# Last image's grams in groups of 32 tokens with turned copies half on VectorE, and fixed places for the second image's grams, in a two-layer attention and correlation kernel

## The chip, the cores and the metric

The kernel runs on one core of one Trainium2 chip. The metric is the device time of one execution in microseconds (us), given as the median of several runs. Profiles come from one further execution, with the hardware profiler on. A core has five engines with an instruction stream each: TensorE (PE in the profile; PEld is its weight loads), VectorE (DVE), ScalarE (ACT), GpSimd (POOL) and SyncE (SP), which here issues nearly all DMAs; SPq in the profile is its queue of DMA issues. Engines wait for each other through semaphores.

## The reference

Input x is 8 images of 768 channels and 32 x 32 tokens, float32. There are two residual layers, each ahead of it a GroupNorm over 32 groups.

```python
x = x + L0(gn(x))
x = x + L1(gn(x))
```

L0 is an attention of 12 heads (64 wide) in which the scores are the outer product of two vectors, the variances of v and of k over the head's 64 channels:

```python
scores = var(v, ddof=1) @ var(k, ddof=1).T * 64 ** -0.5
out = softmax(scores) @ v @ W_proj.T + b_proj
```

L1 divides every token's 768 channels by their norm, correlates each token with 28 neighbours, and puts the 28 correlations behind the 768 channels of a 1x1 convolution:

```python
norm = sqrt(sum(f * f, axis=1)); feat_n = f / max(norm, 1e-12)
corr = [sum(shift(feat_n, r - 3, c - 3) * feat_n, axis=1) for r, c in offsets]
out = einsum('bchw,oc->bohw', concat([f, corr], 1), conv_w) + conv_b
```

The offsets are the two diagonals, the middle row and the middle column of a 7 x 7 square.

## The kernel before, in words

Channels are split into J = 6 blocks of 128 partitions and the 1024 tokens of an image into 8 tiles t of 128 (four rows of 32). The program goes through the images one after the other: keys and values (matmuls `x`, `y`, `z` <- `kv`, L350), attention (`ex` on ScalarE L775, `av` on TensorE L801), the projection, and the 1x1 convolution of the image before (Strassen-like products `x`, `y`, `z` <- `wt`, whose operands `t1f`, `t2f`, `t4f` are made on VectorE). TensorE works through one hand-written order; the correlations of image b - 1 are put beside the keys, values and attention of image b. The last image has nothing beside it: its grams, correlations and products are the end of the program.

**The correlations** are in the class `Corr` (L1126 on). Four steps matter here.

- `turn(t)` (L1130) copies tile t of the feature map `f`, for each side (the left or right 16 columns), so that the 64 tokens of a side lie next to each other: two operations of 128 x 384 elements. For the last image ScalarE does both (`act_copy`, L229), into tiles of `expool` that the attention no longer uses; for the others GpSimd does (L1143), into `turnpool`, which has one buffer. So there turn t + 1 can start when gram t has read turn t.
- `gram(t)` (L1145) multiplies these copies by `f` itself: for each of 6 channel blocks and each side, 64 tokens by the 7 rows x 19 columns around them (133 columns; 76 for t = 7, which has only 4 rows left), added up in one PSUM tile `gr` (L1159). These tiles come from the pool `smp` with two buffers. After its matmuls it starts the turns of the next tile, or of the next two for the last image.
- `out()` (L1169), due 1.65 us later by the planner, copies `gr` into `win` (VectorE; ScalarE for the last image) and writes it to a DRAM buffer `windowed` with one DMA for each side (L1177), 64 partitions at a time. `wins` has two buffers in turns, and a third for t = 7.
- After every four tiles come `diagonals` (four DMAs `dd`, L1191, that read the needed products out of `windowed`), `scale` (`m`, `rn`, `dn`, a transpose `ct` on TensorE, `cr`, four DMAs `rows`, L1228), and after both halves `gather` (14 DMAs, L1239 to L1245, a product on VectorE, three DMAs `cs`<-`cs`, L1254). The matmuls `cc` (L1278, for the last image L1376) then use `cs`.

**What sets the order.** A planner (`Clock`) runs while the program is written: each unit of TensorE's work has a cost in us (`GRAM_US` 1.4, `KV_US` 1.93), and jobs on other engines are due so many us after a unit (`later.after`), or after the planner's VectorE (`later.after_dve`). What is due is written into the program when the planner's time has come, so a cost changes only the order in which instructions stand on each engine. On the chip nothing waits for the planner; each engine runs its instructions in that order.

The grams of image b - 1 are called by `next_to` (L1400), from the attention's steps and from places put into the list of key and value units: `rest.insert`, after 3 and 7 units for images from the third on, and for the second image (whose grams are those of the first) after 7, 12, 14, ... 28. `next_to` runs a gram only once `clock.now` has passed `clock.turned`, which `gram` sets to 1.4 + 2.3 us after its start. `remaining` (L1395) runs those that are left.

For the last image the list is: two product units, the eight grams one after the other, and then the other products, with the `cc` units between the last of them. VectorE meanwhile makes `t1f`, `t2f`, `t4f` and finishes the two products of the image that were set aside (`held<-z,held`, `f<-x,bconv_sb,f`).

Of the kernel before, what the change touches and what calls it, by code (L numbers as in the profile page):

```python
# [13 lines left out]
P = 128  # L14
NB, C, H, W = 8, 768, 32, 32
N = H * W
J = C // P
NH, HD = 12, 64
HP = NH // 2
MT = N // P  # L20
# [7 lines left out]
RUNS = ((0, 0, 4), (31, -1, 3), (62, -2, 5), (93, -3, 7))  # L28
HW = W // 2
TALL, WIDE = MT // 2 + 3, HW + 3  # L30
AHEAD_OF = [o for first, _, count in RUNS for o in range(first, first + count)][1:]
NA = len(AHEAD_OF)
PAD = 99
SPAN = TALL * WIDE
WIN = SPAN + 3
# [18 lines left out]
TAIL = 0.0  # L54
EXP, SUM, STEP_US = 1.07, 1.15, 1.73
KV_US, T_US, CORR_US = 1.93, 2.58, 1.2
GRAM_US, TURN_US = 1.4, 2.3
WARM, BRIDGE = 42, (3, 7)


# [31 lines left out]
class Clock:  # L92


    def __init__(self):
        self.now, self.count, self.jobs = 0.0, 0, []
        self.act, self.rows, self.poll = 0.0, ([], []), lambda: None
        self.dve = self.turned = 0.0

    def after(self, us, job):  # L100
        self.count += 1
# [71 lines left out]
def two_layers(ctx, tc, x, wkv, wproj, bproj, wconv, wcorr, bconv, out):  # L173
# [952 lines left out]
    class Corr:  # L1126
# [3 lines left out]
        def turn(self, t):  # L1130

            last = self.b == NB - 1
            pl, tag = (expool, "ex") if last else (turnpool, "turn")
            flat = pl.tile([P, N if last else J * P], F32, tag=tag, name=f"turn{self.b}_{t}")[:, : J * P]
            self.turned[t] = flat.rearrange("p (j s m) -> p j s m", j=J, s=2)
            to = flat.rearrange("p (j s y x) -> p j s y x", j=J, s=2, x=HW)
            rows = self.f[:, :, t * P : (t + 1) * P].rearrange("p j (y s x) -> p j y s x", y=4, s=2)
            for side in range(2):
                if last:
                    act_copy(0.5, to[:, :, side], rows[:, :, :, side, :])  # L1140
                else:
                    half = rows[:, :, :, side, :]
                    nc.gpsimd.tensor_tensor(to[:, :, side], half, windows(ones, ones.ap[0], (0, J), (HW, 4), (1, HW)), ALU.mult)  # L1143

        def gram(self, t):  # L1145

            b = self.b
            tall = min(TALL, H - 4 * t)
            n = tall * WIDE
            if t not in self.turned:  # L1150
                self.turn(t)
            clock.turned = clock.now + GRAM_US + TURN_US
            block = self.turned[t]
            ps = other([P, SPAN], f"gr{b}_{t}")
            for j in range(J):
                image = self.f[:, j, :].rearrange("p (y x) -> p y x", x=W)
                for side in range(2):
                    left = side * (HW - 3)
                    nc.tensor.matmul(  # L1159
                        ps[side * HD : (side + 1) * HD, :n].rearrange("p (y x) -> p y x", x=WIDE),  # L1160
                        lhsT=block[:, j, side, :],
                        rhs=image[:, 4 * t : 4 * t + tall, left : left + WIDE],
                        start=j == 0, stop=j == J - 1,
                    )
            for ahead in range(t + 1, min(t + (3 if b == NB - 1 else 2), MT)):
                if ahead not in self.turned:
                    self.turn(ahead)

            def out():  # L1169
                win = wins[t % 2 if t < MT - 1 else 2]  # L1170
                if b < NB - 1:
                    vector.tensor_copy(win[:, :n], ps[:, :n])
                else:
                    act_copy(0.3, win[:, :n], ps[:, :n])
                for side in range(2):
                    to = windowed[b % 2][t : t + 1, side * (HD * PITCH + HD - 3) :]
                    nc.sync.dma_start(  # L1177
                        out=windows(to, (HW * PITCH - 3, 4), (PITCH, HW), (1, WIN)), in_=win[side * HD : (side + 1) * HD, :]
                    )
                if t % 4 == 3:  # L1180
                    later.after(4.0, lambda: self.diagonals(t // 4))

            later.after(GRAM_US + 0.25, out)

        def diagonals(self, hf):

# [14 lines left out]
        def scale(self, hf, dd):  # L1201

            b = self.b
            m = st.tile([P, 4], F32, tag="m", name=f"m{b}_{hf}")
            vector.tensor_scalar(m, dd[:, :, 0], NORM_EPS2, None, ALU.max)
            rn = st.tile([P, 4], F32, tag="rn", name=f"rn{b}_{hf}")
            nc.gpsimd.tensor_tensor(rn, m, neghalf, ALU.pow)

            def columns():
                dn = st.tile([P, 4, NROW], F32, tag="dn", name=f"dn{b}_{hf}")  # L1210
                vector.tensor_copy(dn[:, :, 0], rn)
                for q in range(4):
                    vector.scalar_tensor_tensor(dn[:, q, 1:NROW], dd[:, q, :], rn[:, q : q + 1], mask, ALU.mult, ALU.mult)
                later.after_dve(0.7 if b else 5.0 if hf else 7.5, lambda: to_dram(dn))

            def to_dram(dn):
                pt = small(f"ct{b}_{hf}")
                columns, over = dn.rearrange("p q r -> p (q r)"), 4 * NROW - HD
                turned(pt[0:HD, 0:P], columns[:, 0:HD])
                turned(pt[HD:P, 0:P], columns[:, over:])  # L1220
                cr = work([P, P], f"cr{b}_{hf}")
                vector.tensor_copy(
                    cr.rearrange("k (y s x) -> k y s x", y=4, s=2),
                    pt[:, 0:P].rearrange("k (s y x) -> k y s x", s=2, y=4),
                )
                for q in range(4):
                    at, row = PAD + hf * HF + q * P, q * NROW + (HD - over) * (q == 3)
                    nc.sync.dma_start(out=rows[b % 2][:, at : at + P], in_=cr[row : row + NROW, :])  # L1228
                if hf == 1:
                    later.after(3.0, self.gather)  # L1230

            later.after_dve(2.5, columns)
# [161 lines left out]

    def remaining(beside):  # L1395
        while beside:
            clock.turned = 0.0
            next_to(beside)

    def next_to(beside):  # L1400

        if beside and ready.issuperset(beside[0][1]) and clock.now >= clock.turned:
            us, _, unit = beside.pop(0)
            unit()
            clock.pass_time(us)
# [146 lines left out]
    for b in range(NB + 1):  # L1552
# [8 lines left out]
        if b:  # L1561
            has_f = ("f", b - 1),
            if b > 1:
                clock.wait(*has_f, ready=ready)
            f, acc = layer1[b - 1] if b > 1 else first_f * 2
            corr = corrs.pop() if 1 < b < NB else Corr(b - 1, f) if b == NB else None
            conv = Conv(
                b - 1, f, images[b] if b < NB else acc, (lambda b=b: next_image(b + 1)) if b + 1 < NB else lambda: None
            )
            if b < NB:  # L1570

                def low_residual(b=b, f=f):
                    for n in range(JH):
                        later.after(1.5 * n, lambda n=n: nc.sync.dma_start(out=f[:, n, :], in_=xv[b, :, n, :]))

                conv.then = low_residual
            grams = [(GRAM_US if t < MT - 1 else 0.9, has_f if b > 1 else has_f + ("turned",), lambda t=t: (corr or corrs[0]).gram(t)) for t in range(MT)]
            first, start = (0.0, has_f, conv.sums.first), (0.0, (), conv.start)
            if b < NB:
                beside = grams  # L1580
                for n in (3, 7) if b > 1 else (7,) + tuple(range(12, 30, 2)):
                    rest.insert(n, (0.0, has_f, lambda: next_to(beside)))
                rest.insert(len(rest) - 4, (0.0, has_f, lambda: remaining(beside)))
                rest.insert(len(rest) - 4, first)
                rest += [start] + conv.units()
                if b == NB - 1:
                    rest.insert(len(rest) - 3, (0.0, (), conv.set_aside))
            else:
                units, parts = conv.units(), conv.corr_units()
                rest += [first, start] + units[:2] + grams + units[2:17]  # L1590
                for n, unit in enumerate(units[17:]):
                    rest += parts[n : n + 1] + [unit]
        else:
            more = [(us, (("xn", 1),) * (n > 1), unit) for n, (us, _, unit) in enumerate(kv1.units(0))]
            rest.insert(len(rest) - 3, (0.0, (), lambda: apply_second(0)))
            rest += [(0.0, (), lambda: apply_second(1))] + more[:20] + [(0.0, (), lambda: fill_t(3))] + more[20:]
            rest += [(0.0, (), lambda: fill_t(TBLOCKS - 3))]
# [51 lines left out]
```

## Time and profile before

| what | value |
| --- | --- |
| median of 3 runs | 2582.31 us (2581.68 to 2583.05) |
| the profiled execution: time | 2580.96 us |
| its span | 2579.2 us |
| TensorE busy in it | 2571.7 us, 14798 matmul instructions |
| VectorE / ScalarE / GpSimd busy | 1586.1 / 1418.3 / 424.4 us |
| last image's eight grams (first `gr` to first `y`) | 2510.96 to 2522.19 us of the span |
| mean granted TensorE clock | 1.000 |

How to read it: the span is the time from the first to the last instruction of the profiled execution, and every time inside the trace counts from its start. One float32 matmul of the program shows as two instructions of TensorE in the profile. A line such as `L350 PE MATMUL x<-kv,xn 128*64 128x384 f32 x1512 | 260.3, 486 | 0.0` is a group of instructions: source line, engine, operation, output and inputs by the program's names, shape (here 128 rows by 64 columns of weights, 384 columns moved), their number, total busy us, mean ns of one, and idle time of the engine ahead of them. Lines of a timeline have start us, duration us, what, the number of merged instructions, and in brackets the idle time ahead of it with what ended it. Matmuls are pipelined: one's duration is longer than the distance to the next one's start, so sums are made from start to start.

### The profile page before, as it was taken

Reading aid. Unit: us, or ns where it says so; the run is one execution under the profiler, and the core shown is the slowest. Engines: PE = TensorE matmul, PEld = TensorE weight load, DVE = VectorE, ACT = ScalarE, POOL = GpSimd, SP = SyncE. Lnnn points to the kernel's source line nnn. Section 1 sums busy time; section 2 is a strip of 40 time slices with the busy share of each in tenths; the row PEclk is TensorE's granted clock in tenths of the full one; section 3 lists DMA queues with packets and bytes.
Section 4 is the critical chain, followed back from the end, with each engine's and each line's share of the span. In section 5 each row is a group of like instructions: output and inputs, shape, how many; then the busy total and the mean of one; then the engine's idle time right before and its main releaser. Section 6 shows DMA issues by size and latency. Waiting matters only on the chain.

```text
span 2579.2 us, 40704 instructions
## 1 busy us (share of the span) xinstructions
PE 2571.7 (100%) x14798; PEld 1328.9 (52%) x14798; DVE 1586.1 (61%) x4101; ACT 1418.3 (55%) x1972; POOL 424.4 (16%) x449
## 2 busy tenths in 40 slices
PE   9999999999999999999999999999999999999999
PEld 5654356434764345643476434764347643575333
DVE  6868735775447853478534885358853577536864
ACT  1497279811697217971179711897118971189610
POOL 4320130004300043000430003300133001331000
PEclk9999999999999999999999999999999999999999
DMA  8766356355563655636556365563655636545333
GB/s 293 291 225 224 104 204 194 116 198 170 184 202 104 197 168 176 206 99 205 170 175 202 97 211 170 167 203 105 220 170 163 207 106 219 167 139 166 118 111 108
DMA packets 324718, 448.19 MB, mean 174 GB/s; under 512 B 59810, under 2 KB 245522, under 8 KB 324518
## 3 DMA queue, kind: packets, MB, share of 16 engines
q1 hardware_dynamic: 322454, 442.24, 53.1%
q10 hardware_dynamic: 2064, 3.34, 0.4%
q8 instruction: 118, 1.93, 0.3%
q14 instruction: 82, 0.67, 0.1%
HBM read 376.70 MB, written 64.40 MB: 171 GB/s over the span
## 4 chain that ended last, share of the span: by engine, by line
PE 97%; DMA 1%; ACT 1%; DVE 0%; SPq 0%; issue 0%; POOL 0%; ACTq 0%; POOLq 0%; DVEq 0%
PE x L350 34%; PE av L801 25%; PE y L350 17%; PE z L350 10%; PE own L350 5%; PE gr L1159 3%; PE den L832 1%; ACT ex L775 1%; PE warm L419 1%; DMA bc<-vdr 1%; ACT junk L785 0%; PE z L1064 0%; PE y L1064 0%; PE cc L1278 0%; DMA vdr<-rsv 0%
## 5 line engine op out<-in xcount | busy, mean ns | idle before, releaser
L775 ACT ACTIVATE ex<-bc,nk 128x1024 f32<-128x1024 f32 x768 | 826.9, 1137 | 398.8 <-DMA bc<-vdr 167.2
L801 PE MATMUL av<-ex,v 128*64 128x512 f32 x3072 | 694.2, 593 | 1.6 <-ACT ex L775 1.5
L801 PEld LDWEIGHTS av<-ex,v 128*64 128x64 f32 x3072 | 328.6, 137 | 322.7 <-issue 211.4
L785 ACT ACTIVATE junk<-bk,vm 128x1024 bf16<-128x1024 f32 x368 | 420.4, 1142 | 28.0 <-issue 10.7
L167 DVE TENSOR_TENSOR acc<-acc,ex 128x1024 f32<-128x1024 f32 x300 | 344.8, 1211 | 0.0
L350 PE MATMUL y<-kv,s 128*64 128x384 f32 x1488 | 265.3, 487 | 0.1
L350 PE MATMUL x<-kv,xn 128*64 128x384 f32 x1512 | 260.3, 486 | 0.0
L350 PE MATMUL x<-kv,s 128*64 128x384 f32 x1488 | 256.0, 486 | 0.0
L229 ACT COPY kp<-x 128x384 f32<-128x384 f32 x28 | 13.3, 478 | 404.7 <-PE x L350 395.9
L350 PEld LDWEIGHTS x<-kv,xn 128*64 128x64 f32 x1512 | 139.2, 137 | 104.6 <-issue 85.7
L350 PEld LDWEIGHTS x<-kv,s 128*64 128x64 f32 x1488 | 143.0, 137 | 92.7 <-issue 72.5
L350 PEld LDWEIGHTS y<-kv,s 128*64 128x64 f32 x1488 | 137.2, 137 | 88.6 <-issue 72.4
L530 POOL TENSOR_TENSOR rstda<-vea,neghalf 128x1 f32<-128x1 f32 x8 | 4.8, 595 | 950.8 <-DVE vea L167 950.8
L1143 POOL TENSOR_TENSOR turn<-f,ones 128x384 f32<-128x384 f32 x112 | 111.0, 1011 | 247.1 <-PE gr L1159 169.0
L350 PE MATMUL z<-kv,xn 128*64 128x384 f32 x768 | 134.2, 486 | 0.0
L350 PE MATMUL x<-f,wt 128*64 128x512 f32 x504 | 118.8, 592 | 0.0
L167 DVE TENSOR_TENSOR v<-y,v 128x128 f32<-128x128 f32 x180 | 40.9, 282 | 121.7 <-PE y L350 121.6
L636 POOL TENSOR_TENSOR s<-xn 128x384 f32<-128x384 f32 x64 | 65.0, 1026 | 293.3 <-PE x L350 181.7
L167 DVE BATCH_NORM_STATS2 vbn<-v 128x6 f32<-128x64 f32 x720 | 101.5, 209 | 0.0
L350 PEld LDWEIGHTS z<-kv,xn 128*64 128x64 f32 x768 | 75.0, 137 | 46.7 <-issue 36.1
L229 ACT COPY acc<-li 32x256 f32<-32x256 f32 x128 | 51.5, 402 | 82.9 <-DVE li L167 81.5
L1159 PEld LDWEIGHTS gr<-f,turn 128*64 128x64 f32 x1344 | 88.0, 136 | 11.9 <-issue 5.1
(205 smaller groups left out, 3132.5 us busy)
## 6 DMA issues: line engine op xcount, KB each, us to landing
kv<-kvs SPq DMA_DIRECT2D x124, 576.0 KB
kv<-in_wkv_dram SPq DMA_DIRECT2D x95, 576.0 KB
bc<-vdr SPq DMA_DIRECT2D x96, 512.0 KB
f<-in_x_dram SPq DMA_DIRECT2D x48, 512.0 KB
bk<-kdr SPq DMA_DIRECT2D x46, 512.0 KB
x1d<-f SPq DMA_DIRECT2D x42, 512.0 KB
xn<-x1d SPq DMA_DIRECT2D x42, 512.0 KB
out_dram<-xn SPq DMA_DIRECT2D x82, 256.0 KB
```

The source lines that it names most:

```text
L167: return getattr(self.engine, name)(*args, **kw)
L229: nc.scalar.copy(to, at)
L350: nc.tensor.matmul(out[at], lhsT=lhsT[:, at], rhs=rhs, start=start, stop=stop, **kw)
L419: nc.tensor.matmul(warm[:, 0:P], lhsT=ident, rhs=ident, start=True, stop=True)
L530: nc.gpsimd.tensor_tensor(self.rstd, ve, neghalf[:, 0:1], ALU.pow)
L636: nc.gpsimd.tensor_tensor(self.sums[g][:, 0], a[g][2], a[g][3], ALU.add)
L775: nc.scalar.activation(ex, self.bc[e], AF.Exp, scale=self.kv.nk[self.half][:, h, t : t + 1])
L785: nc.scalar.activation(junk, self.bk[e], AF.Exp, scale=self.kv.m2[self.half][:, h, t : t + 1], accum_out=self.sums[:, e, t : t + 1],)
L801: nc.tensor.matmul(self.av[hf][e * HD : (e + 1) * HD, :], lhsT=self.vt[:, t, e, :], rhs=exs[e][:, hf * HF : (hf + 1) * HF], start=t == 0, ...
L832: nc.tensor.matmul(den[at * 32 : (at + 1) * 32, :], lhsT=ones[:, 0:32], rhs=self.acc[e][:, hf * HF : (hf + 1) * HF], start=True, stop=True,)
L1143: nc.gpsimd.tensor_tensor(to[:, :, side], half, windows(ones, ones.ap[0], (0, J), (HW, 4), (1, HW)), ALU.mult)
L1159: nc.tensor.matmul(ps[side * HD : (side + 1) * HD, :n].rearrange("p (y x) -> p y x", x=WIDE), lhsT=block[:, j, side, :], rhs=image[:, 4 * ...
```

## The change

For the last image a gram is made in four groups of 32 tokens (two rows of one side) rather than two of 64. Each group needs only 5 rows x 19 columns = 95 columns of `f` rather than 133 (76 as before for t = 7), so there are 24 matmuls rather than 12 in a gram. The window of each group starts at its own first row, and for t = 0 to 6 `win` is written by four DMAs of 32 partitions (2 x 16 x 98 elements) rather than two of 64 (4 x 16 x 136). The turned copy of the right side (`side` 1) is made on VectorE rather than ScalarE. In the planner a gram of the last image is 0.3 us cheaper, its `out` is due 0.3 us earlier and its `to_dram` 1.7 rather than 0.7 us after its columns.

For all images the gate `clock.turned` is gone, and the second image's grams stand after 7, 11 and 15 units of its keys and values, with the others from the attention's steps and `remaining`.

```diff
+SHORT = 2 + 3
-GRAM_US, TURN_US = 1.4, 2.3
+GRAM_US = 1.4
...
             for side in range(2):
-                if last:
+                if last and side:
+                    vector.tensor_copy(to[:, :, side], rows[:, :, :, side, :])
+                elif last:
                     act_copy(0.5, to[:, :, side], rows[:, :, :, side, :])
...
         def gram(self, t):
             b = self.b
-            tall = min(TALL, H - 4 * t)
+            last = t == MT - 1
+            groups = 4 if b == NB - 1 else 2
+            tall = min(SHORT if groups == 4 else TALL, H - 4 * t)
             n = tall * WIDE
             if t not in self.turned:
                 self.turn(t)
-            clock.turned = clock.now + GRAM_US + TURN_US
...
-                for side in range(2):
-                    left = side * (HW - 3)
+                each = P // groups
+                for at in range(groups):
+                    side, low = divmod(at, groups // 2)
+                    left, first = side * (HW - 3), 4 * t + (0 if last else 2 * low)
                     nc.tensor.matmul(
-                        ps[side * HD : (side + 1) * HD, :n].rearrange("p (y x) -> p y x", x=WIDE),
-                        lhsT=block[:, j, side, :],
-                        rhs=image[:, 4 * t : 4 * t + tall, left : left + WIDE],
+                        ps[at * each : (at + 1) * each, :n].rearrange("p (y x) -> p y x", x=WIDE),
+                        lhsT=block[:, j, side, low * each : (low + 1) * each],
+                        rhs=image[:, first : first + tall, left : left + WIDE],
                         start=j == 0, stop=j == J - 1,
                     )
...
-                for side in range(2):
-                    to = windowed[b % 2][t : t + 1, side * (HD * PITCH + HD - 3) :]
+                whole = last or groups == 2
+                size, count, down = (WIN, 4, 0) if whole else (SHORT * WIDE + 3, 2, 2 * (HW * PITCH - 3 + WIDE))
+                for first in range(0, P, count * HW):
+                    side, low = divmod(first, HD)
+                    to = windowed[b % 2][t : t + 1, side * (HD * PITCH + HD - 3) + (down if low else 0) :]
                     nc.sync.dma_start(
-                        out=windows(to, (HW * PITCH - 3, 4), (PITCH, HW), (1, WIN)), in_=win[side * HD : (side + 1) * HD, :]
+                        out=windows(to, (HW * PITCH - 3, count), (PITCH, HW), (1, size)),
+                        in_=win[first : first + count * HW, :size],
                     )
...
-            later.after(GRAM_US + 0.25, out)
+            later.after(GRAM_US + 0.25 - (0.3 if b == NB - 1 else 0.0), out)
...
-                later.after_dve(0.7 if b else 5.0 if hf else 7.5, lambda: to_dram(dn))
+                later.after_dve((0.7 if b < NB - 1 else 1.7) if b else 5.0 if hf else 7.5, lambda: to_dram(dn))
...
     def remaining(beside):
         while beside:
-            clock.turned = 0.0
             next_to(beside)
...
-        if beside and ready.issuperset(beside[0][1]) and clock.now >= clock.turned:
+        if beside and ready.issuperset(beside[0][1]):
...
-                for n in (3, 7) if b > 1 else (7,) + tuple(range(12, 30, 2)):
+                for n in (3, 7) if b > 1 else (7, 11, 15):
```

More of the change, by code (lines that the diff above doesn't have):

```diff
@@ L97, in __init__ @@
         self.act, self.rows, self.poll = 0.0, ([], []), lambda: None
-        self.dve = self.turned = 0.0
+        self.dve = 0.0
     def after(self, us, job):
@@ L1576, in two_layers @@
                 conv.then = low_residual
-            grams = [(GRAM_US if t < MT - 1 else 0.9, has_f if b > 1 else has_f + ("turned",), lambda t=t: (corr or corrs[0]).gram(t)) for t in range(MT)]
+            grams = [(GRAM_US - (0.3 if b == NB else 0.0) if t < MT - 1 else 0.9, has_f if b > 1 else has_f + ("turned",), lambda t=t: (corr or corrs[0]).gram(t)) for t in range(MT)]
             first, start = (0.0, has_f, conv.sums.first), (0.0, (), conv.start)
```

## The prediction

> **What bounds the kernel now.** I read the totals first, then the chain of work that ended last, then the same chain in the stretch of the last image's grams, and then each engine's timeline there and in the second image. TensorE is busy for 2571.7 of 2579.2 us, and the page's chain says the same:
>
> ```profile
> PE 97%; DMA 1%; ACT 1%; DVE 0%; SPq 0%; issue 0%; POOL 0%; ACTq 0%; POOLq 0%; DVEq 0%
> ```
>
> So an edit counts only where it shortens TensorE's work or makes it wait. The chain from 2508 to 2530 us (start, us, what) is the last image's grams:
>
> ```profile
> 2511.12 2.75 PE gr L1159 x48
> ...
> 2517.91 0.28 ACT win L229
> 2518.19 0.02 issue
> 2518.21 0.52 SPq L1177
> 2518.72 0.05 issue
> 2518.78 2.15 DMA windowed<-win
> ...
> 2521.03 0.28 ACT win L229
> 2521.30 0.04 issue
> 2521.35 1.01 PE gr L1159 x24
> 2522.36 5.15 PE y L350 x24
> ```
>
> The reader is to see that this stage hangs partly on the windows: a copy to `win`, two issues 0.57 us apart (2518.21, 2518.78; the piece called DMA starts with the second), landing 1.63 us after the second ends, then the next copy into that buffer, which frees a PSUM tile for a gram. By start times on TensorE the grams run from 2510.96 to 2522.19 = 11.23 us. Seven grams at 1.36 and one at 0.79 make 10.31, so 0.92 us is waiting.
>
> **1. The shorter grams.** A pair of 64-column matmuls starts 113.3 ns after the last at 133 columns and 66 ns at 76; on that line 95 columns take 82 ns. A gram is then 12 rounds x 82 = 0.98 us, if four 32-column groups run beside each other as two 64-column ones do. The row for that form:
>
> ```profile
> 2420.40 1.06 PE L832 MATMUL den<-acc,ones 128*32 128x512 f32 x8
> ```
>
> Two rounds of four at 512 columns take 1.0 us (the rounds start 0.453 apart, the four within 20 ns), so the groups do run together; some 0.13 us goes on entering the form and as much on leaving. The eight grams would be 7 x 0.98 + 0.79 + 0.29 = 7.94 us: at best 3.3 us less than 11.23, with no waits left. The Trainium skill speaks against it: "TensorE: Matmul & The Clock Gate", section "Wait — 56ns, not 53.3ns?", has starts never closer than some 25 ns, which would make a round 100 ns and the best gain (my estimate from it) 1.7 us. The den records, 6.7 ns apart in a round, do not show that floor.
>
> **2. Half the turned copies on VectorE.** Before, ScalarE made the first turned copies while it had nothing else to do:
>
> ```profile
> 2508.43 3.40 ACT L229 COPY turn<-f_last 128x384 f32<-128x384 f32 x8 [49.85 <-DVE f_last L167]
> ```
>
> VectorE has no such gap (timeline, same stretch):
>
> ```profile
> 2511.26 0.74 DVE L167 SCALAR_TENSOR_TENSOR f<-x,bconv_sb,f 128x512 f32<-128x512 f32 x1
> 2511.92 1.88 DVE L167 TENSOR_TENSOR t2f<-f_last,t1f 128x512 f32<-128x512 f32 x3
> 2513.72 0.74 DVE L167 SCALAR_TENSOR_TENSOR f<-x,bconv_sb,f 128x512 f32<-128x512 f32 x1
> 2514.39 1.89 DVE L167 TENSOR_TENSOR t<-f_last 128x512 f32<-128x512 f32 x3
> ```
>
> In the new order on VectorE the first three copies stand behind t2f, that is at 2513.72, and everything ahead of it runs without a pause. A 128x384 copy takes 0.55 us (the mean of kp<-x, which reads PSUM); taken. Its bounds are 0.27, by a 128x1024 f_last at 0.72 to 0.81, and 0.93, the pair of ScalarE copies. So the copy is there at 2514.28, and gr_0, whose third matmul reads it, runs from about 2514.35 instead of 2510.96: **TensorE stands for 3.4 us**, which is all that the shorter grams can return. ScalarE's 8 x 0.41 us less is worth nothing by itself.
>
> **3. Four issues for each gram instead of two.** The queue's own rows (ns min/median/max):
>
> ```profile
> L1177 SPq DMA_DIRECT2D windowed<-win x128: 511/526/622, 354.3 to 2527.8; - x128
> L1228 SPq DMA_DIRECT2D rows<-cr x64: 294/322/1336, 396.7 to 2539.7; - x64
> L1243 SPq DMA_DIRECT2D cs<-rows x32: 231/270/288, 423.1 to 2547.9; - x32
> ```
>
> No row has the new shape (2x16x98). Bounds: 0.30 from start to start by cs<-rows, 0.62 by the slowest windowed. I take 0.55: it is a windowed write with one dimension shorter, so that row is nearest. Then SyncE needs 4 x 0.55 = 2.2 us for a gram against 0.98 of TensorE: **the queue becomes the bound of the stage.** gr_0 ends at 2514.35 + 0.98 + 0.13 = 2515.46; 0.51 us later (as between gr_0 and its first issue before) the first write is issued, 2515.97. The window of gram 5 goes into the buffer of gram 3, whose last issue ends 16 x 0.55 = 8.8 us later; landing, copy and release add 1.63 + 0.42 = 2.05, and gr_7 can start at 2526.82 where it started at 2521.35: **+5.5 us** on all that follows. At 0.62 it is +6.6; at 0.30 the landing of each buffer's writes sets the pace instead, first issue + 12 x 0.30 + 4.1, about +2.3.
>
> **4. Behind it.** The wt load and the four dd issues that stand behind 28 window issues are later, as is the ct transpose (to_dram due at 1.7, not 0.7; one pair of matmuls later). gather's last load lands near 2556 and is wanted near 2560. The cs product goes behind one more f<-z on VectorE; the copies of cs before landed at 2559.1 and the first cc started at 2561.35, and about 0.2 of this 2.25 us is left. Taken as nothing, at worst 0.5 us.
>
> **5. The second image.** With one buffer, turn t+1 starts only when gram t has read turn t. POOL's rows beside keys and values:
>
> ```profile
> 373.69 1.99 POOL L1143 TENSOR_TENSOR turn<-f,ones 128x384 f32<-128x384 f32 x2 [3.25 <-PE gr L1159]
> 375.63 1.97 POOL L636 TENSOR_TENSOR s<-xn 128x384 f32<-128x384 f32 x2
> ...
> 383.32 1.99 POOL L1143 TENSOR_TENSOR turn<-f,ones 128x384 f32<-128x384 f32 x2
> 385.25 1.04 POOL L1207 TENSOR_TENSOR rn<-m,neghalf 128x4 f32<-128x4 f32 x1
> 387.15 1.99 POOL L1143 TENSOR_TENSOR turn<-f,ones 128x384 f32<-128x384 f32 x2 [0.86 <-PE gr L1159]
> ```
>
> A gram's end to its turn takes 0.70, the turn 1.99, the next gram follows 0.06 later: 2.75 us to cover. With the gate gone gr_0, gr_1 and gr_2 each have one unit between them, y<-kv and then x<-kv, 1.935 us each: two stalls of 0.82. gr_3 to gr_5 have an attention step or two units (3.87) and are covered. turn_5 now stands ahead of the eight s operations (7.7 us) and turn_6 behind them, which I work out to leave gr_6 some 0.3 us short. On the other side ScalarE's order changes: two of its sums (junk, 1.27 each) move up, one into this wait for bc:
>
> ```profile
> 446.74 4.43 ACT L775 ACTIVATE ex<-bc,nk 128x1024 f32<-128x1024 f32 x4 [2.89 <-DMA bc<-vdr]
> ...
> 461.70 1.69 PE L801 MATMUL av<-ex,v 128*64 128x512 f32 x4 [0.24 <-ACT ex L775]
> ```
>
> ScalarE's six ex from 460.51 come 1.27 us earlier, and the 0.57 us that TensorE's starts lose ahead of the second line go. Sum: 2 x 0.82 + 0.3 - 0.57 = **+1.4 us**; bounds -0.6 (no stall) and +2.7 (the stalls, a longer one at gr_6, and no gain).
>
> **The sum.** 5.5 + 1.4 = +6.9 us on the profiled execution's 2580.96 (span 2579.2 and 1.76 around it) is 2587.9. That execution is 1.35 us under the median 2582.31, so against the median: **2589.2 us**, +0.27%. A measurement of this kernel can tell 0.2%, 5.2 us, from no change.
>
> **Rivals.**
> A. The smaller write is cheap to issue, 0.30 to 0.37 us: step 3 then gives +2.3 to +3.3, and with step 5 the sum is +1.5 to +5, about 2586. For it: three-row loads at 0.27. Against: the windowed row hardly varies (511 to 622 ns). The second image's stalls being covered (step 5 at -0.6 to 0) ends here too: 5.5 - 0.3 = +5.2 or less.
> B. TensorE, 45% busy in the queue-bound stage (0.98 of 2.2) after standing 3.4 us, loses its clock. The window at the end of the span (us, PE busy, ..., PEclk, DMA share, GB/s) has it:
>
> ```profile
> 2575.00:2579.20 4.20, 0.39 (x2) 0.00 (x0) 0.75 (x1) 0.00 (x0) 0.00 (x0) 0.85 0.18 68
> ```
>
> The records there go from full to half clock at 2577.98, 2.6 us after the last matmul. Two to three us of that clock fall under issues anyway; then some 3.4 to 6.8 us of Strassen products run at half speed, 1.7 to 3.4 us more: +8.6 to +11.7, about 2592. Against: each gap inside the stage is only 1.2 us. The skill's rule in Part 1 of the same page (half clock after an idle window of about 3.4 us, free-running) would give this or not by the phase of the window.
> C. Not slower: the copy on VectorE does not hold gr_0. Its place in VectorE's order decides; were turn_0 made ahead of t1f, as ScalarE's is (done by 2509.2), and an issue under 0.25 us (four of them under a gram's 0.98), 11.23 would become 7.94. With 461.70's 0.57 gained: -3.3 to -3.9 us, about 2578.7. Against: the order puts three operations and t2f ahead of it, and no issue row is that cheap.
>
> **Chances.** Forecast (+5.2 to +8.6) 0.55; A 0.24; B 0.13; C 0.08. The forecast and B are slower by over 0.2%: 0.68. A and half of C are within: 0.28. The other half of C, with gains that I do not see, is faster: 0.04. The range reaches from A's lower part (+1.7) to the end of B (+11.7): 2584.0 to 2594.0; it leaves out C and the ends of A and B, under 0.2. The forecast's own range is 2587.5 to 2590.9.
>
> **What would show it.** Right: gr_0's third matmul released by DVE turn near 2514.3; rows windowed x4 gapless on SyncE, 0.5 us or more each; grams near 1.0 us but 2.2 apart; y from about 2527.7; two waits for POOL turn of 0.8 us near 355 to 360. Wrong: windowed rows under 0.4; grams longer than 1.2; y before 2524; a PEclk under 1.00 between 2511 and 2535.

## The result, and the profile after

The changed kernel took 2586.98 us (median of 21 runs), the kernel before 2581.14 us (21 runs): ratio **1.0021, interval 1.0015 to 1.0028**, slower by 3.9 to 7.2 us. The profiled execution has a span of 2583.6 us (2579.2 before). It is the fastest of the 21 (2585.32 us), and its mean granted clock is 1.000; of the other 20 executions, two have 1.000, fifteen 0.999 and three 0.998.

To see where that comes from I took the start of every matmul in both traces and subtracted before from after, instruction by instruction. The difference is -0.96 us behind the warm-up (the granted clock rises to 1.00 at 5.66 us there, and at 7.75 in before) and -0.70 at 340 us, -2.02 at 350, -1.23 at 400, -2.0 to -2.2 from 470 to 2500, and +4.35 from the first y behind the last image's grams to the end. So +6.36 us arose in the last image's grams (6.21 between the first gram's start and the first y). In the second image +0.79 arose beside the keys and values and -0.84 near 461 us; the -1.32 between 342 and 350 lies ahead of every instruction that the change moves there (see e1 and e2).

The chain that ended last, in the last image's grams of the changed kernel (start us, us, what):

```profile
2511.79 0.28 DVE turn L168
2512.07 0.04 issue
2512.11 1.20 PE gr L1165 x46
...
2513.60 0.68 SPq L1186
...
2522.59 0.57 SPq L1186
2523.16 0.04 issue
2523.20 1.97 DMA windowed<-win
...
2525.27 0.25 ACT win L230
2525.51 0.04 issue
2525.56 1.00 PE gr L1165 x48
2526.56 5.30 PE y L351 x24
```

Between 2513.60 and 2523.16 it holds only issues on SyncE's queue, 15 of them; the 16th starts at 2523.20 and is the first part of the piece called DMA. They are those of four windows. Where before two issues stood in the chain between grams, now the queue is the chain. TensorE's waits from 2508 to 2530 us (waiting line, for what: us in total, times, longest) show the two costs side by side, and a short stop that comes back in e11 and e12:

```profile
PE gr L1165 <- ACT win L230: 5.0, 4, 1.3
PE gr L1165 <- DVE turn L168: 2.7, 1, 2.7
PE gr L1165 <- issue: 0.4, 1, 0.4
```

The timelines of VectorE and SyncE there:

```profile
2509.91 1.88 DVE L168 TENSOR_TENSOR t2f<-f_last,t1f 128x512 f32<-128x512 f32 x3
2511.71 0.89 DVE L168 COPY turn<-f_last 128x384 f32<-128x384 f32 x3
```

```profile
2513.60 17.73 SPq L1186 DMA_DIRECT2D windowed<-win  x28
```

The copies stand behind t2f without a pause, and the 28 issues take 17.73 us without one: 0.63 us each, four to a gram. The windows of the trace by stretch (us, PE busy, PEld, DVE, ACT, POOL busy, PEclk, DMA share, GB/s) have the clock at 1.00 in this execution, although TensorE was busy for only 8.98 of 14.5 us (e1, e3 and e4 show others):

```profile
2512.00:2526.50 14.50, 8.98 (x382) 7.78 (x382) 6.39 (x15) 3.18 (x10) 0.00 (x0) 1.00 0.10 25
```

In the second image GpSimd's turns come at 3.75 us from each other while each gram has only one unit behind it, and TensorE waits for them twice:

```profile
352.04 1.98 POOL L1146 TENSOR_TENSOR turn<-f,ones 128x384 f32<-128x384 f32 x2 [4.78 <-PE gr L1165]
355.79 1.98 POOL L1146 TENSOR_TENSOR turn<-f,ones 128x384 f32<-128x384 f32 x2 [1.77 <-PE gr L1165]
359.54 1.98 POOL L1146 TENSOR_TENSOR turn<-f,ones 128x384 f32<-128x384 f32 x2 [1.77 <-PE gr L1165]
```

### The profile page after: what moved, and what is told of

The parts are those of the page before. It is cut to its first block, busy times and chain, and to the rows that moved or that the text cites. A ratio compares the mean times of both kernels' runs of the same rounds, so it can differ in the third digit from the quotient of the medians.

```text
span 2583.6 us, 41108 instructions
## 1 busy us (share of the span) xinstructions
PE 2569.0 (99%) x14990; PEld 1328.2 (51%) x14990; DVE 1587.8 (61%) x4109; ACT 1415.4 (55%) x1964; POOL 424.8 (16%) x449
## 4 chain that ended last, share of the span: by engine, by line
PE 98%; DVE 1%; SPq 0%; POOL 0%; issue 0%; ACT 0%; DMA 0%; POOLq 0%; ACTq 0%; DVEq 0%
PE x L351 35%; PE av L802 25%; PE y L351 18%; PE z L351 10%; PE own L351 5%; PE gr L1165 3%; PE den L833 1%; PE warm L420 1%; SPq L1186 0%; PE y L1065 0%; PE cc L1288 0%; PE z L1065 0%; DVE acc L168 0%; DVE f_last L168 0%; POOL turn L1146 0%
## 5 line engine op out<-in xcount | busy, mean ns | idle before, releaser
L1165 PEld LDWEIGHTS gr<-f,turn 128*64 128x64 f32 x1344 | 88.9, 136 | 12.1 <-issue 3.3
```

The lines of the kernel that those rows point to most:

```text
L1165: nc.tensor.matmul(ps[at * each : (at + 1) * each, :n].rearrange("p (y x) -> p y x", x=WIDE), lhsT=block[:, j, side, low * each : (low + 1 ...
```

## The experiments

My theory after the result: in the last image VectorE's copies and the four issues a gram, one behind the other, cost more than the shorter grams return; the second image's new order is worth about nothing. The rivals stand with each run. "Stage" is from the first gram's start to the first y: 11.24 us before, 17.45 after.

**e1: only the last image's part** (gate, `TURN_US` and places of the second image as before).

```diff
-                for n in (3, 7) if b > 1 else (7, 11, 15):
+                for n in (3, 7) if b > 1 else (7,) + tuple(range(12, 30, 2)):
```

> Only the last image's part of the change; the second image's grams are placed and gated as before. Theory (the last image's stage alone makes the change slower; the second image's new order is worth nothing): from the first gram's start to the first y takes 17.4 us as in the changed kernel (11.2 before), so +6.3 us on before, ratio 1.0024, and no wait for a turned copy of GpSimd near 354 us. Rival (the second image's new order itself saves the 1.3 us by which the changed kernel's trace runs ahead of before's between 340 and 480 us): this kernel is 1.3 us slower than the changed one against the same before. If the stall of 1.45 us ahead of av near 349.6 is there in this execution and not in others with the same order, it belongs to the execution and not to the order.

Ratio 1.0024 (1.0015 to 1.0034), stage 18.0 us, +6.9 us behind it: the theory, and 0.6 us more than in after, of which 0.37 lie in gr_7 itself (1.37 us against 1.00). Here the clock did fall. These are gr_5 and gr_6 of e1, the same 48 instructions each:

```profile
2522.06 1.19 PE L1166 MATMUL gr<-f_last,turn 128*32 128x95 f32 x48 [1.32 <-ACT win L230]
2524.58 2.13 PE L1166 MATMUL gr<-f_last,turn 128*32 128x95 f32 x48 [1.33 <-ACT win L230]
```

The granted clock of this trace is 0.50 from 2514.28 to 2517.69 us and from 2524.52 to 2527.93, 3.41 us each; gr_7 starts in the second stretch. In e3 it is 0.50 from 2518.90 to 2522.31, in e4 from 2514.23 to 2517.64. In the 3.41 us ahead of each of the four stretches TensorE was busy for 0.82 to 1.24 us, by the profile's modelled ends. Cut into stretches of 3.41 us in step with the clock's changes, all fourteen traces have it busy for 1.39 us (e8) or more in every other stretch between the warm-up and the last matmul, and behind those the clock stayed at 1.00.

The stall ahead of av near 349 us, 1.45 us in before's trace, is 0.36 here with the same order: it belongs to the execution.

**e2: only the second image's part** (the kernel before without the gate and with places 7, 11, 15).

> Only the second image's part: gate removed, grams after 7, 11 and 15 units; the last image as before. Theory: two waits for turned copies of GpSimd of about 0.5 and 0.4 us near 354 and 358 us, and one of 0.3 us ahead of the transposes behind gr_6, against some 0.9 us saved near 461 us, where ScalarE's ex come earlier: sum between -0.2 and +0.2 us from 350 to 480 us, time as before. Rival (the new order itself saves 1.3 us): ratio 0.9995. What was predicted: +1.4 us, ratio 1.0005.

Ratio 0.9996 (0.9988 to 1.0005), that is -3.1 to +1.3 us: -1.3 cannot be told from none, and +1.4 lies at the edge. The trace is finer. The grams beside keys and values cost +0.80 us. But TensorE's stall near 461 us, which I had expected to go, was longer, 1.74 us in starts, and 1.17 us were lost there against before. This is ScalarE's line ahead of it, in e2:

```profile
448.71 4.44 ACT L775 ACTIVATE ex<-bc,nk 128x1024 f32<-128x1024 f32 x4 [5.32 <-DMA bc<-vdr]
```

The wait for bc was 2.89 us in before, 3.15 in after and 5.32 here. All thirteen traces besides before's, in us against before:

| order of the second image | traces | grams beside keys and values | near 461 us, mean (range) |
| --- | --- | --- | --- |
| new | after, e2, e3, e4, e5, e8 | +0.79 to +0.80 | -0.31 (-0.84 to +1.17) |
| old | e1, e6, e7, e9, e10, e11, e12 | -0.01 to +0.01 | +0.96 (+0.21 to +2.18) |

The +0.79 is the order's own. The loss near 461 us varies with the landing of bc; the new order has it lower by 1.3 us on average (1.15 with before itself, at 0, among the old ones), about as much as one of ScalarE's sums (1.27). Together the second image's part is worth some -0.4 to -0.5 us on average. By the scatter of these few traces that mean has a standard error of about 0.4 us, so it cannot be told from nothing; nor could the times of e2 show it. From 342 to 350 us all thirteen are earlier than before's trace, by 0.57 to 1.60 us, in both orders.

**e3: both turned copies on ScalarE.**

```diff
-                if last and side:
-                    vector.tensor_copy(to[:, :, side], rows[:, :, :, side, :])
-                elif last:
+                if last:
```

> The changed kernel with both turned copies of the last image on ScalarE again. Theory (two costs one behind the other, the queue's pace the larger): gr_0 does not wait, everything in the stage starts 2.7 us earlier, but the 28 window issues stay 0.62 us apart and the windows 2.5 us, so the stage takes 17.4 - 2.7 = 14.7 us, 3.5 more than before. Rival (the copies on VectorE are the cause, the issues follow the grams): the stage takes 8 to 11 us, no more than before.

Stage 14.4 us, 3.3 more than before by the starts behind it; ratio 1.0014 (1.0005 to 1.0023). gr_0 does not wait, and the queue keeps its pace (SyncE's timeline of e3):

```profile
2512.17 17.74 SPq L1184 DMA_DIRECT2D windowed<-win  x28
```

The windows stay 2.5 us apart, also where the granted clock is 0.50, so the queue hid that stretch. VectorE's place is worth 3.0 us of the 6.36, and without it the kernel is still slower than before.

**e4: half the window writes left out** (those of every second group of 32).

```diff
-                for first in range(0, P, count * HW):
+                for first in range(0, P, HD if b == NB - 1 else count * HW):
```

> The changed kernel without the window writes of every second group of 32 in the last image (14 issues instead of 28 for tiles 0 to 6; half of the windows stays unwritten, so the correlations of that image are wrong). Theory (the queue sets the pace): issues keep 0.6 us each whatever the number, gr_0 still waits 2.7 us for VectorE, then the landing of each buffer's writes sets the pace, first y near 13.2 us after the first gram (17.4 in the changed kernel, 11.2 before). Rival (the grams or the copies into win are slower than thought, not the queue): the stage stays at 16 us or more.

Stage 13.9 us: 3.6 less than in after, between theory and rival and near the theory; gr_0 still waited for VectorE. The theory's 13.2 is not tested cleanly: the granted clock was 0.50 over the first grams, and the three took 4.48 us from the end of that wait (2513.06 to 2517.54), against 2.96 in after. An issue of the 2x16x98 write took 0.57 us here too, where the queue had pauses between pairs. So the price goes with the write and not with a full queue; the larger 4x16x136 write takes 0.52. Which of its sizes makes the smaller one dearer no run separates.

**e5 and e6: two cures.** Side 1 is copied by GpSimd; a gram's two lower groups are copied a second time inside `win`, two rows lower, so that two DMAs write a window as before; e6 has four buffers of `win` for the last image and the old second image.

```diff
-                if last and side:
-                    vector.tensor_copy(to[:, :, side], rows[:, :, :, side, :])
-                elif last:
+                if last and not side:
...
                     act_copy(0.3, win[:, :n], ps[:, :n])
-                whole = last or groups == 2
+                    for at in () if last else (HD // 2, HD + HD // 2):
+                        act_copy(0.2, win[at : at + HD // 2, 2 * WIDE : 2 * WIDE + n], ps[at : at + HD // 2, :n])
+                whole = True
```

> The changed kernel with two cures: side 1 of the last image's turned copies on GpSimd, and each window shifted inside win by two small ScalarE copies, so that two DMAs of 4x16x136 write it as before; two buffers of win. Theory (queue and VectorE were the two costs, the shorter grams themselves are as worked out): gr_0 does not wait, the landing of each buffer's writes now sets the pace, the stage takes 10.0 to 10.6 us (17.4 in the changed kernel, 11.2 before), about 0.9 us less than before. Rival (groups of 32 hold the stage up in some other way): 12 us or more.

> As e5, with four buffers of win for the last image, and the second image's grams gated and placed as before. Theory: nothing waits any more, the eight grams take 8.0 to 8.4 us as worked out, 3 us less than before: ratio 0.9988 to 0.9990, faster than both kernels. Rival (the three copies of ScalarE a gram take over as the bound): 9.5 us or more.

Stages 12.1 and 12.0 us; e6's ratio 1.0002 (0.9993 to 1.0011). Both theories fell. In e6 buffers and queue no longer bind (in e5 two grams still waited for copies into `win`, 0.8 us in all); GpSimd does, and it takes VectorE along. e6's rival had named ScalarE's copies instead. TensorE, GpSimd and VectorE in e6:

```profile
2513.68 1.19 PE L1169 MATMUL gr<-f_last,turn 128*32 128x95 f32 x48 [1.20 <-POOL turn L1149]
```

```profile
2507.45 13.28 POOL L1149 TENSOR_TENSOR turn<-f_last,ones 128x384 f32<-128x384 f32 x8 [4.30 <-DVE f_last L168]
```

```profile
2513.35 3.67 DVE L168 TENSOR_TENSOR t<-f_last 128x512 f32<-128x512 f32 x3
```

Eight turns at 1.66 us on average, where one beside keys and values takes 1.0, and three t in 3.67 us, where before they took 1.89. In the records the two engines take turns from 2513.6 us on, an operation each; ahead of that the first and third turn took 2.5 and 2.7 us while VectorE kept its pace. The Trainium skill, "SBUF — State Buffer", section "🔬 SBUF: two separate sides", has it so: one port pair is held by one of the two engines for a whole instruction.

**e7 and e10: the kernel before with four buffers of `win`, nothing else** (e10 is e7 again, timed).

```diff
+            self.wins = wins[0:2]
+            if b == NB - 1:
+                self.wins = [bcpool.tile([P, N], F32, tag="bc", name=f"lastwin{n}")[:, :WIN] for n in range(4)]
...
-                win = wins[t % 2 if t < MT - 1 else 2]
+                win = self.wins[t % len(self.wins)] if t < MT - 1 else wins[2]
```

> The kernel before with four buffers of win for the last image and nothing else. Theory: the 0.9 us of waiting for windows goes, the stage takes 10.3 to 10.5 us; what e6 has beyond that is from the shorter grams. Rival (the waits come from the queue, not from the buffers): 11 us.

> The kernel of e7 again, timed: 0.7 us less in the last image's stage by the trace of e7, ratio 0.9997; too little to be told from no change if the interval is as wide as in the other runs.

Stage 10.53 us in both, -0.70 in both, and not a wait left:

```profile
2509.89 10.70 PE L1164 MATMUL gr<-f_last,turn 128*64 128x133 f32 x192
```

Ratio in e10 0.9996 (0.9987 to 1.0004).

**e8: as e6, but side 1 on VectorE as in the change, and the new second image.**

> As e6 (two DMAs a gram, four buffers) but with side 1 of the turned copies on VectorE as in the change, and the second image's new order. Theory (the copies' place in VectorE's order costs 2.7 to 3.1 us by itself): gr_0's third matmul waits for it as in the changed kernel, and the stage takes 10.8 to 11.4 us, all of the shorter grams' gain spent. Rival (the wait hides behind the windows): 8 to 9.5 us.

Stage 12.8 us, more than either expected. VectorE's place costs its 3 us by itself, and then ScalarE sets the pace, with one turned copy and three window copies a gram, 1.32 us (TensorE, then ScalarE, in e8):

```profile
2514.15 3.27 PE L1170 MATMUL gr<-f_last,turn 128*32 128x95 f32 x140 [3.03 <-DVE turn L168]
```

```profile
2516.35 0.52 ACT L230 COPY turn<-f_last 128x384 f32<-128x384 f32 x1 [0.17 <-PE gr L1170]
2516.89 0.76 ACT L230 COPY lastwin<-gr 128x95 f32<-128x95 f32 x3
```

**e9: the first six tiles' turned copies made before t1f on both engines, on top of e8, old second image.**

```diff
+                early = (0.0, has_f, lambda: [corr.turn(t) for t in range(6)])
-                rest += [first, start] + units[:2] + grams + units[2:17]
+                rest += [early, first, start] + units[:2] + grams + units[2:17]
```

> The change's groups of 32 and its copies half on VectorE, but with the first six turned copies ahead of t1f on both engines, windows shifted inside win and written by two DMAs, four buffers of win, and the second image as before. In e8 ScalarE was the bound (one turned copy and three window copies a gram, 1.32 us) and VectorE's copies stood behind t2f; in e6 GpSimd's copies were. Theory (with these three costs away the shorter grams come through): gr_0 does not wait, the stage takes 8.2 to 9.0 us, 2.2 to 3.0 less than before, ratio 0.9988 to 0.9991. Rival (another resource takes over again: ScalarE's three copies, or the queue at 1.24 us a gram): 9.5 to 10.5 us, no better than e7.

Stage 10.4 us, the rival's figure; ratio 0.9994 (0.9985 to 1.0003). gr_0 started at 2512.94, but the first window was issued at 2517.24, and two grams waited 1.3 us for the copies into `win` behind it. On the queue the write of held stands ahead of the windows, and held now came behind six copies:

```profile
2514.75 1.76 SPq L1406 DMA_DIRECT2D out_dram<-held  x2
2516.60 0.53 SPq L338 DMA_DIRECT2D wt<-tsc  x1
2517.24 8.63 SPq L1194 DMA_DIRECT2D windowed<-lastwin  x14
```

**e11: the copies behind held and ahead of t1f** (`[start] + units[:1] + [early, first] + units[1:2] + grams`).

> As e9, but VectorE finishes held first, makes the six turned copies, and only then t1f. In e9 the copies came ahead of held, and the write of held, which stands ahead of the windows on SyncE's queue, held the first window back to 4.3 us after gr_0's start. Theory (the order on the queue was e9's only cost): first window issue 2.0 to 2.3 us after gr_0's start, the stage takes 8.2 to 8.8 us, some 2.7 less than before, ratio 0.9989 to 0.9990. Rival (ScalarE's copies, the queue or the buffers bind next): 9.5 to 10.4 us.

Stage 10.0 us, ratio 0.9997 (0.9987 to 1.0006). The queue's pause is gone (first issue 1.9 us after gr_0), and the theory still missed: gr_5 waits 0.41 us for ScalarE, and TensorE stood 0.63 us inside gr_3 for nothing that the profile shows.

**e12: the last two turned copies off ScalarE too.**

```diff
-                if last and side:
+                if last and (side or t > 5):
```

> As e11, but the last two turned copies of side 0 (tiles 6 and 7) on VectorE too, so that ScalarE has only its three window copies (0.76 us a gram) from gr_0 on. In e11 its copy for tile 6 stood ahead of the window copies of gram 3 and made gr_5 and the grams behind it wait. Theory (ScalarE was what was left in e11): the stage takes 9.0 to 9.4 us (10.0 in e11, 11.2 before; the 0.6 us in which TensorE stands within gr_3 for nothing that the profile shows stays), ratio 0.9991 to 0.9993. Rival (buffers or queue): 9.7 to 10.0 us.

Stage 10.5 us, ratio 0.9997 (0.9988 to 1.0006): theory and rival both missed. No wait for any engine, buffer or queue is left, and the chain is this:

```profile
2511.24 4.21 PE gr L1171 x189
2515.45 0.85 issue
2516.30 3.31 PE gr L1171 x126
2519.60 0.64 issue
2520.24 1.48 PE gr L1171 x67
2521.71 4.44 PE y L351 x19
```

TensorE itself stops twice. Between the two stops lie 126 matmuls and as many weight loads, 252 instructions. The instruction queue's line for 2511 to 2523 us (loads, MB, share of the DMA engines), first in before, then in e12:

```profile
q8 instruction: 2, 0.03, 1.2%
```

```profile
q8 instruction: 3, 0.05, 1.9%
```

Its loads are of 16384 bytes, 65 bytes for each of the 252 instructions ("Perfetto Trace Analysis" of the Trainium skill, section "The 4-stage abstract model", has instructions of 64 bytes). Over the whole trace of before there are 118 such loads for 30185 instructions on TensorE (14798 matmuls, as many weight loads, and 589 of its sequencer), 256 for each load. In e12 two of them ended at 2514.85 and 2518.87, and TensorE went on 1.45 and 1.37 us later.

The first of these stops comes at the 190th matmul instruction of the grams. At that same instruction TensorE stopped in after, e3, e9 and e11 too (0.20 to 0.88 us from start to start), and went on 1.30 to 1.45 us after the load had ended; in after that lay in the shade of the queue. In e1, e4, e5, e6 and e8, where the load had ended 1.44 to 2.82 us before that instruction's start, there is no stop. That TensorE ran out of instructions fits all ten traces; no run moved the load alone, so it is argued and not shown.

## Why the prediction was right, and where it was not

The forecast was 2589.2 us against a median of 2582.31, +6.9 us; the measured difference is +5.8 us between the medians, +3.9 to +7.2 by the interval. As a time, 2586.98 lies 0.5 us under the forecast's own range (2587.5 to 2590.9) and nearer to rival A's 2586, since before's median came out at 2581.14; it is the traces that tell the two apart. The mechanism of the last image held. Step 3 was 0.9 us too small and step 5 some 1.8 us too large, and that these errors partly cancel is luck.

- **Step 1, the shorter grams**: 82 ns a round and 0.98 us a gram were predicted and are in the trace (gr_1). The floor of some 25 ns a start that the prediction cites from the Trainium skill does not show: the four starts of a round lie within 20 ns. The gain of up to 3.3 us was not reached by any run: the best stage with groups of 32 was 10.0 us (e11), with 1.1 us less behind it than before, and 0.5 less than 64-token groups with four buffers.
- **Step 2, VectorE's copies**: place and wait as predicted. A copy took 0.35 us alone and 0.27 from start to start, the low bound, not 0.55; gr_0 waited 2.7 us by the profile, and it went on 3.07 us after its first start, not 3.4.
- **Step 3, four issues a gram**: the formula held, the issue was undersized. 0.57 us and 0.05 between, with 0.05 more at each gram, make 0.62 to 0.63 and not 0.55; 16 of them, the first two at 0.68 and 0.65, took 10.17 us (2513.60 to 2523.77) and not 8.8. With the upper bound the step's own figure was +6.6; measured +6.36 for steps 1 to 3.
- **Step 4**: nothing was lost behind it; the difference is +4.35 us from the first y on to the end.
- **Step 5, the second image, was the term that missed**: +1.4 was predicted; the means over traces give -0.4 to -0.5 with a standard error of about 0.4, so the sign is open, but it is not +1.4. The stalls cost 0.79 us in all and not 1.94: the two were 0.51 and 0.43 us and not 0.82, because the cycle from one gram to the next was 3.75 us and not 1.36 + 2.75 = 4.11. And the gain near 461 us, 0.57 by the one trace I had, is 1.2 to 1.3 between the means of the two orders, and varies from execution to execution by 2 us.
- **Rivals**: A fell (the smaller write was dearer, not cheaper). B happened, but not at its price: the clock stayed at 1.00 in the profiled execution, but fell to 0.50 in e1, e3 and e4, whose grams wait in much the same way, and 18 of the changed kernel's 21 executions have a mean clock under 1.000. In the three traces the half clock ended ahead of the first y, so it fell on grams that mostly waited anyway (0.37 us in gr_7 of e1, none seen in e3) and not on the products; no execution took more than 2588.64 us, where B had 2590.9 to 2594. C's place was the right one (VectorE's order), but with it mended neither the queue nor, later, TensorE let the 3.3 us through.

## What to carry to other kernels

Halving the work of an instruction on the busiest engine pays only if everything that is done once for each piece (an issue on a queue, a copy, and by inference an instruction fetched) has room for twice as many; here each of them was at its limit in turn. One more pair of buffers gave the kernel before two thirds of the best gain, by the traces (0.70 of 1.07 us); the times of neither can be told from before's. When an operation moves to another engine, look where it lands in that engine's order, and whose operation it pushes back: in e9 the copies cost nothing themselves, but a write behind them held up a queue. A stall that a single trace shows behind a DMA's landing is not a fixed price; take its range over several traces. The same holds for the clock: the one profiled execution seemed to rule rival B out, and the traces of three experiments have it.

## What the runs showed of the hardware

- A DMA issue of 2x16x98 from 32 partitions took 0.57 us, one of 4x16x136 from 64 partitions 0.52: less data, more time.
- GpSimd's copy with two SBUF inputs beside VectorE's tensor_tensor: 1.66 us on average instead of 1.0, and VectorE's 1.2 to 1.4 instead of 0.6 where the two alternate (e6).
- Four 32-column matmuls run beside each other at 82 ns a round for 95 columns. Where nothing else held them (e12), TensorE stopped for 0.85 us after 189 of these instructions and for 0.64 us after 126 more.
- The granted clock was 0.50 for 3.41 us behind a stretch of 3.41 us in which TensorE was busy for 0.82 to 1.24 us (e1 twice, e3, e4), and 1.00 behind those with 1.39 us (e8), 1.60 us (after) and more.
- With one order of the second image, the stalls behind the landing of bc near 461 us differ by up to 2 us between executions; before's 21 runs lie between 2578.8 and 2585.2 us. Of 92 further executions of before, timed with e1 to e12, the 10 with a mean granted clock of 0.999 took 2582.5 to 2585.4 us and the 82 with 1.000 took 2578.6 to 2583.6; which comes first, a stall or the clock, is not shown.
